# Layer 3's attention in a four-layer fp32 kernel: probabilities turned in 32x32 blocks on VectorE and placed by DMA over DRAM, values by 128 columns, order of the last heads' output

## The chip, the cores and the metric

The kernel runs on one core of one Trainium2 chip, all in fp32. The metric is the device time of one execution in microseconds. Before the change it is 3037.99 us, the median of 17 runs (3025.1 to 3042.96). Engines are named PE (TensorE; PEld are its weight loads), DVE (VectorE), ACT (ScalarE), POOL (GpSimd) and SP (SyncE, which here issues DMAs).

## The reference

Four layers, each `x = x + attention(xn) + ffn(xn)` with `xn` the layer norm of `x`: 2048 tokens of 256 values. The layers differ (a state-space mixer, latent attention with product keys, attention with few keys and a mixture of experts, and the last one). The change concerns layer 3, whose two parts are full attention with 16 heads of 128 on 4 sequences of 512 tokens, and a mixture of 8 experts:

```python
q = jnp.einsum('bpd,hde->bphe', x, W_Q) + b_Q          # k, v alike
scores = jnp.einsum('bqhe,bkhe->bhqk', q, k) / ATTN_SCALE
scores = jnp.where(causal, scores, IGNORE)
attn = jax.nn.softmax(scores, axis=-1)
z = jnp.einsum('bkhe,bhqk->bqhe', v, attn)
out = jnp.einsum('bqhe,hed->bqd', z, W_O) + b_O
# experts: out += (silu(x @ gate.T) * (x @ up.T)) @ down.T * w[:, e]
```

## The kernel before, in words

`layer3` (L2080) weaves three generators: the attention (`full_attention`, L1405), the rest of layer 2, and near the end the router of the experts. When they are done, the experts run (`SevenProductGlus.pieces`, L468). `weave` (L501) takes the next piece from the stream that is furthest behind by the costs that the pieces yield. What the pieces trace is then ordered for each engine by the tile framework, from its own estimate of when operands are ready; `tc.keep_in_program_order` pins an instruction behind the one that was traced just before it on its engine. Every engine, SP's queue of DMAs too, then runs its list in order.

The attention goes through 64 heads, n = 0 to 63 (L1555): four groups g of four heads, in each group the four sequences b, in each of these the four heads h = n mod 4. In its turn a head n does this:

- with h = 0, the values V of four heads (`values_of`, L1491): two groups of seven products of 256 columns
- the products of the next head's q and k: seven products of 256 columns each (`SevenProducts`, L282; p1 to p7 are placed by hand between the other pieces)
- the scores in four rows i of 128 queries, causal, so of 128, 256, 384 and 512 columns (`exp_scores`, L942): a matmul (L949), a DVE pass for scale, mask and minimum (L952), the exponential with its sum on ACT (L956), then reciprocal and scaling on DVE (`probabilities`, L1514, L1517 and L1518)
- for the head before it (`last`): the probabilities turned with keys on partitions (`turned`, L1521): ten 128x128 turns on PE into PSUM of tag "tr" (L1531), four copies by DVE into `PT` (L1532)
- for the head before that (`second`): the values (`values`, L1534), four matmuls of 512, 384, 256 and 128 columns (L1539), copied to `zT` by ACT (L1544); with h = 3 also the output product of four heads (`heads_out`, L960: 16 products of 256 columns, added to x by DVE at L151)

So the order on PE is, for a head without V and without output product: p1, the values of `second`, p4 of the head before, p5, the turns of 512 columns, p2, p6, then row by row scores, turns of `last`, p3 and p7. PSUM has eight banks: four of tag "mm", two of "tr", two of "acc" (`ps`, L47).

SP loads the weights of a group (`load`, L53 for wu and L1427 for wo), and waits on its queue until their places are free. Nothing else of the attention uses DMA.

The experts' stage (L468) runs 64 steps of seven products for gate and up, and interleaves the down products of the steps before as jobs (`down`, L453, `SevenSummed`, L348; each product is added to x by DVE at L461). The four last jobs follow one after the other. `hidden_sums` (L421) makes its sums on POOL.

Of the kernel before, what the change touches and what calls it, by code (L numbers as in the profile page):

```python
# [1 line left out]

# [1 line left out]

# [11 lines left out]
P = 128  # L16
# [209 lines left out]
HALF = SEQ // 2  # L226


def right_sums(c, out, blocks):

    sub = c.nc.gpsimd.tensor_sub
    (b11, b12), (b21, b22) = blocks
    sub(out[0], b12, b11)
    sub(out[1], b22, out[0])
    sub(out[2], b22, b12)
    sub(out[3], b21, out[1])
# [152 lines left out]
class SevenProductGlus:  # L391
# [26 lines left out]
        )  # L418
        return [[v[:, q, :] for v in sums] for q in range(2)]

    def hidden_sums(self, hT, q):  # L421


        t = [self.c.tile(self.pool, [P, SEQ], "hidden_sums", bufs=13) for _ in range(4)]
        (b11, b12), (b21, b22) = [[hT[half][2 * q + k] for half in range(2)] for k in range(2)]
        right_sums(self.c, t, [[b11, b12], [b21, b22]])
        hT[2].append([b11, b21, b22] + t)

    def start(self, u, p, k, hT):
# [20 lines left out]
        right = self.tokens.right(2 * p, 2)  # L450
        return SevenProducts(c, pool, left, right, out, (2, HALF), ("mm", "mm", "tr"))

    def down(self, u, p, j, hT):  # L453
# [12 lines left out]
        return SevenSummed(c, self.units[u][1], right, add, P, ("acc", "acc", "tr"))  # L466

    def pieces(self, pool):  # L468

        self.pool = pool  # L470
        n_units = len(self.srcs)
        order = [(u, p, k) for u in range(n_units) for p in range(NB // 2) for k in range(4)]
        last, jobs = None, []
        for n in range(len(order) + 6):
            now = None
            if n < len(order):
                u, p, k = order[n]
                if (p, k) == (1, 0) and u + 1 < n_units:
                    self.load(u + 1)
                if k == 0:  # L480
                    hT = [[], [], []]
                now = self.start(u, p, k, hT), u, p, k, hT
            job = self.down(*jobs.pop(0)) if jobs else None
            for mine, name, other in zip(
                (now, last, now, now, last, now, now), ("p1", "p7", "p5", "p2", "p4", "p6", "p3"),
                SevenSummed.ORDER,
            ):
                if mine:
                    getattr(mine[0], name)()
                    yield 0.87  # L490
                if job:
                    getattr(job, other)()
                    yield 0.45
                if mine and name == "p4" and mine[3] % 2 == 1:
                    self.hidden_sums(mine[4], mine[3] // 2)
            if last and last[3] == 3:
                jobs += [(*last[1:3], j, last[4]) for j in range(4)]
            last = now


def weave(c, *streams, flush=True):  # L501
# [455 lines left out]
    return pr  # L957


def heads_out(c, zT, wo, b):  # L960

    for t in range(TPB):
        po = c.ps("acc")[:, :DM]
        for h in range(4):
            c.nc.tensor.matmul(  # L965
                po, lhsT=zT[:, h, t * P : (t + 1) * P], rhs=wo[:, h, :],
                start=(h == 0), stop=(h == 3),
            )
        add_scaled(c, b * TPB + t, po)

# [434 lines left out]
def full_attention(c, a, sums, tokens):  # L1405
# [5 lines left out]
    with ExitStack() as stack:  # L1411
# [4 lines left out]
        bias = c.tile(keep, [P, 48 + DM], "bias")  # L1416
        nc.sync.dma_start(bias, a["f_small"])
        late = late_mask(c, keep, 1.0)
        units = {}

        def load(g):
# [21 lines left out]
        def projections(n):  # L1443


            g, b, h = n // 16, n // 4 % 4, n % 4
            hh = 4 * g + h
            q, k = c.tile(pool, [P, SEQ], "q"), c.tile(pool, [P, SEQ], "k")

            def out(which, bank, part):  # L1450
                to = (q, k)[which // 2][:, which % 2 * HALF : (which % 2 + 1) * HALF]
                col = which // 2 * 16 + hh
                shift = bias[:, col : col + 1]
                if part is None:
# [6 lines left out]
            return q, k, SevenProducts(c, pool, left, right, out, (HALF,))  # L1461

        def plain_projections(h):

# [26 lines left out]
        def values_of(g, b):  # L1491


            V = c.tile(pool, [P, TPB, 4, P], "V")
            right = tokens.right(b)

            def group(t):
                def out(which, bank, part):
                    col = which // 2 * 2
                    to = V[:, which % 2 * 2 + t, col : col + 2, :].rearrange("p h d -> p (h d)")  # L1500
                    if part is None:
                        nc.scalar.copy(to, bank)
                    else:
                        nc.vector.tensor_add(to, bank, part)

                return SevenProducts(
                    c, pool, units[g][2], [v[:, 0, t * P : (t + 1) * P] for v in right], out,
                    (DM,), ("mm", "mm", "acc"), swap=True,
                )

            groups = [group(t) for t in range(2)]
            return V, groups

        def probabilities(q, k, i):  # L1514
            rinv = c.tile(pool, [P, 1], "rinv", bufs=4)
            pr = exp_scores(c, pool, late, q, k, i, rinv, -scale, tc.keep_in_program_order)
            nc.vector.reciprocal(rinv, rinv)  # L1517
            nc.vector.tensor_scalar_mul(pr, pr, rinv)  # L1518
            return pr

        def turned(head, i):  # L1521

            if head is None:
                return
            if i == TPB - 1:
                head["PT"] = c.tile(pool, [P, TPB, SEQ], "PT")
            PT, pr, n = head["PT"], head["prs"][i], (i + 1) * P
            pt = c.ps("tr")
            for j in range(i + 1):
                cols = slice(j * P, (j + 1) * P)  # L1530
                tc.keep_in_program_order(nc.tensor.transpose(pt[:, cols], pr[:, cols], c.ident))  # L1531
            nc.vector.tensor_copy(PT[:, : i + 1, i * P : n], v3(pt[:, :n], P))  # L1532

        def values(head):  # L1534

            h, zT = head["h"], head["zT"]
            z = c.ps("acc")
            for j in range(TPB):
                tc.keep_in_program_order(nc.tensor.matmul(  # L1539
                    z[:, j * P :], lhsT=head["V"][:, j, h, :], rhs=head["PT"][:, j, j * P :],  # L1540
                    start=(j == 0), stop=(j == TPB - 1),
                ))
            hh = head["hh"]
            nc.scalar.activation(zT[:, h, :], z, AF.Identity, bias=bias[:, 32 + hh : 33 + hh])  # L1544
            yield 2.1
            if h == 3:
                heads_out(c, zT, head["wo"], head["b"])
                if hh == 15:
                    c.part_done(head["b"])
                yield 6.8  # L1550

        load(0)
        value_sums(0)
        second = last = None
        for n in range(64):  # L1555
            g, b, h = n // 16, n // 4 % 4, n % 4
            hh = 4 * g + h
# [7 lines left out]
            if h == 0:  # L1565
# [14 lines left out]
                zT = c.tile(pool, [P, 4, SEQ], "zT", bufs=1)  # L1580
                if b == 3 and g < 3:
                    load(g + 1)
            if (h, b) == (1, 3) and g < 3:
# [5 lines left out]
                    yield 1.7  # L1589
            else:  # L1590
                q, k, _ = ahead
            head = dict(h=h, hh=hh, b=b, V=V, zT=zT, wo=units[g][3], prs=[])
            now = None
            if 3 <= n < 63:
                ahead = projections(n + 1)
                now = ahead[2]
            if tail:
                turned(last, 3)
                yield 0.45
                for group in tail:  # L1600
                    group.p4()
                    yield 0.45
            if now:
                now.p1()
                yield 0.45
            if second:
                yield from values(second)
            if late_group:
                late_group.p4()
                yield 0.45  # L1610
            if now:
                now.p5()
                yield 0.45
            if not tail:
                turned(last, 3)
                yield 0.45
            if now:
                now.p2()
# [2 lines left out]
                yield 0.45  # L1621
            for i in range(TPB):
                head["prs"].append(probabilities(q, k, i))
                if i < 3:
                    turned(last, 2 - i)
                yield 0.7
                if now and i < 2:
                    (now.p3, now.p7)[i]()
                    yield 0.45
            second, last = last, head  # L1630
        turned(last, 3)
        yield from values(second)
        for i in range(3):
            turned(last, 2 - i)
        yield from values(last)

# [668 lines left out]
```

## Time and profile before

| what | value |
|---|---|
| median of 17 runs | 3037.99 us |
| the profiled execution's own time | 3035.4 us |
| its span, first to last instruction | 3033.6 us |
| mean granted clock of TensorE | 0.993 |
| layer 3's attention | about 1645 to 2437 us of the span |
| experts | about 2437 to 3031 us |
| DVE copies of turned rows, 128 / 256 / 384 / 512 columns (L1532) | 283 / 419 / 557 / 691 ns |
| scaling by the reciprocal, same widths (L1518) | 279 / 418 / 437 / 515 ns |
| DVE pass over the scores, same widths (L952) | 290 / 417 / 540 / 681 ns |
| exponential, same widths (L956) | 401 / 508 / 616 / 723 ns |

A row of the timeline gives start, length and what ran. Matmuls overlap, so the price of one is the step from its start to the next start, not its length. An fp32 matmul other than a turn is two instructions. "[0.96 <-DVE PT L1532]" behind a row means that its engine sat idle for 0.96 us before it, until that instruction was done. Of a DMA issue the profile gives the median time from issue to landing. The stretch view gives each engine's busy time in a stretch, the clock that TensorE was granted (1.00 is full) and what the DMAs did.

### The profile page before, as it was taken

How to read it: one execution, taken by the hardware profiler on the slowest of the kernel's cores; microseconds unless marked ns; L12 is line 12 of the kernel's file. 1: busy time of each engine (PE TensorE's matmuls, PEld its weight loads, DVE VectorE, ACT ScalarE, POOL GpSimd, SP SyncE). 2: the span in 40 equal slices, each digit the busy share in tenths (PEclk: the TensorE clock that was granted, in tenths of full speed). 3: DMA queues.
4: the chain of work that ended last, by engine and by line, in shares of the span. 5: the costliest groups of instructions: out<-in, count | busy, mean ns of one | idle time of the engine just before them, and what ended most of it. 6: DMA issues, size and time to landing. Idle time of an engine off the chain costs nothing.

```text
span 3033.6 us, 39747 instructions
## 1 busy us (share of the span) xinstructions
PE 2974.7 (98%) x13674; PEld 1962.8 (65%) x13674; DVE 2119.9 (70%) x5366; ACT 1399.9 (46%) x3336; POOL 916.9 (30%) x749
## 2 busy tenths in 40 slices
PE   8999999999999999999998999999999999999999
PEld 5666666666655555556676677777777756666666
DVE  5877877787787788787665766666666756666665
ACT  4444544444466666666523444444444433333332
POOL 0665555556210132331235200010010034333332
PEclk9999999999999999999999999999999999999999
DMA  3333333232221244443234000000000000000000
GB/s 133 94 108 122 99 97 117 85 122 88 87 66 37 64 125 102 111 105 113 85 102 128 15 1 28 1 22 8 1 21 1 22 1 22 21 21 21 22 1 29
DMA packets 89114, 185.39 MB, mean 61 GB/s; under 512 B 14192, under 2 KB 57216, under 8 KB 84176
## 3 DMA queue, kind: packets, MB, share of 16 engines
q1 hardware_dynamic: 74448, 135.05, 13.7%
q0 software_dynamic: 14176, 47.01, 6.2%
q8 instruction: 108, 1.77, 0.2%
q14 instruction: 94, 0.77, 0.1%
q10 hardware_dynamic: 288, 0.79, 0.1%
HBM read 160.92 MB, written 12.98 MB: 57 GB/s over the span
## 4 chain that ended last, share of the span: by engine, by line
PE 84%; DVE 8%; DMA 2%; ACT 2%; POOL 2%; issue 1%; SPq 0%; ACTq 0%; DVEq 0%; POOLq 0%
PE mm L301 19%; PE mm L134 14%; PE mm L949 7%; PE acc L301 6%; PE acc L1539 5%; PE acc L965 4%; PE tr L787 3%; PE tr L301 3%; PE tr L1531 2%; PE tr L1076 2%; PE mm L142 2%; PE tr L212 2%; PE acc L1212 2%; PE acc L765 2%; PE acc L212 2%; PE mm L1930 1%
## 5 line engine op out<-in xcount | busy, mean ns | idle before, releaser
L956 ACT ACTIVATE pr<-pr,nm 128x128 f32<-128x128 f32 (+3 forms) x512 | 286.3, 559 | 262.2 <-DVE nm L952 258.3
L312 ACT COPY part<-mm 128x256 f32<-128x256 f32 (+1 forms) x462 | 208.7, 459 | 231.9 <-PE mm L301 229.0
L301 PE MATMUL mm<-token_sums,unit_sums 128*128 128x512 f32 (+1 forms) x744 | 303.2, 490 | 0.0
L134 PE MATMUL mm<-xnT,wu 128*128 128x512 f32 x624 | 293.7, 608 | 3.7 <-DVE nm L952 3.6
L1330 POOL DMA_INDIRECT e<-in_p_experts,ids x128 | 129.8, 1014 | 473.9 <-DVE x L152 336.5
L952 DVE CUSTOM_DVE_ANT_0 pr<-mm,late 128x128 f32<-128x128 f32 (+3 forms) x512 | 245.4, 482 | 21.5 <-PE mm L949 18.8
L134 PE MATMUL mm<-xnT,w_in 128*128 128x512 f32 x512 | 229.2, 593 | 0.6 <-DVE cy L555 0.6
L461 DVE SCALAR_TENSOR_TENSOR x<-acc,cw,x 128x128 f32<-128x128 f32 x384 | 132.9, 346 | 112.5 <-PE acc L301 110.4
L134 PEld LDWEIGHTS mm<-xnT,wu 128*128 128x128 f32 x624 | 117.0, 195 | 127.5 <-issue 111.6
L555 DVE SCALAR_TENSOR_TENSOR cy<-mm,ws,cy 128x509 f32<-128x509 f32 (+2 forms) x216 | 160.1, 744 | 51.6 <-ACT cy L551 47.6
L949 PE MATMUL mm<-kf,qf 128*128 128x128 f32 (+3 forms) x512 | 177.1, 446 | 4.4 <-DVE qf L1053 3.8
L949 PE MATMUL mm<-k,q 128*128 128x128 f32 (+3 forms) x512 | 177.7, 436 | 1.2 <-DVE q L1478 1.2
L725 POOL TENSOR_TENSOR G<-G,CB 128x1024 f32<-128x1024 f32 x64 | 151.4, 2366 | 82.3 <-DVE G L688 76.2
L708 ACT ACTIVATE xD<-xc,ws 128x128 f32<-128x128 f32 x256 | 83.9, 390 | 193.1 <-POOL y L749 183.8
L301 PEld LDWEIGHTS acc<-down_sums,hidden_sums 128*128 128x128 f32 x768 | 114.8, 191 | 86.6 <-issue 83.7
L1532 DVE COPY PT<-tr 128x512 f32<-128x512 f32 (+3 forms) x256 | 124.6, 487 | 62.0 <-PE tr L1531 60.1
L134 PEld LDWEIGHTS mm<-xnT,w_in 128*128 128x128 f32 x512 | 96.5, 190 | 104.3 <-issue 94.7
L1539 PE MATMUL acc<-PT,V 128*128 128x512 f32 (+3 forms) x512 | 153.8, 444 | 5.0 <-DVE PT L1532 5.0
L688 DVE TENSOR_TENSOR_SCAN G<-G,eye 128x1024 f32<-128x1024 f32 x64 | 148.2, 2315 | 0.0
L1539 PEld LDWEIGHTS acc<-PT,V 128*128 128x128 f32 x512 | 93.9, 191 | 71.7 <-issue 31.7
L301 PE MATMUL mm<-xnT,wu 128*128 128x256 f32 (+1 forms) x368 | 137.0, 454 | 0.0
L444 DVE TENSOR_TENSOR whole<-mm,part 128x512 f32<-128x512 f32 x128 | 88.5, 692 | 68.4 <-PE mm L301 68.3
(408 smaller groups left out, 6720.5 us busy)
## 6 DMA issues: line engine op xcount, KB each, us to landing
G<-own SPq DMA_DIRECT2D x64, 512.0 KB, 4.2
w_in<-in_m_units SPq DMA_DIRECT2D x16, 1024.0 KB, 5.0
eb<-since SPq DMA_DIRECT2D x96, 128.0 KB, 3.3
wu<-in_o_units SPq DMA_DIRECT2D x8, 1536.0 KB, 6.4
wo<-in_m_units SPq DMA_DIRECT2D x16, 512.0 KB, 3.8
psw<-pes SPq DMA_DIRECT2D x128, 64.0 KB, 2.7
wu<-in_g_units SPq DMA_DIRECT2D x4, 1536.0 KB, 6.7
wu<-in_f_units SPq DMA_DIRECT2D x4, 1536.0 KB, 7.8
```

The lines of the kernel that those rows point to most:

```text
L134: c.nc.tensor.matmul(out, lhsT=w[:, d, cols], rhs=c.xnT[:, d, tokens], start=(d == 0), stop=(d == 1))
L301: self.c.tc.keep_in_program_order(self.c.nc.tensor.matmul(bank, lhsT=lhsT, rhs=rhs, start=first, stop=True, skip_group_check=not first))
L312: self.c.nc.scalar.copy(r, bank)
L461: c.nc.vector.scalar_tensor_tensor(x, bank, self.factor(u, tt), x, ALU.mult, ALU.add)
L555: nc.vector.scalar_tensor_tensor(y[:, j:], src[:, : SEQ - j], conv[:, k, 3 - j : 4 - j], y[:, j:], ALU.mult, ALU.add,)
L688: tc.keep_in_program_order(nc.vector.tensor_tensor_scan(flat, flat, eye.rearrange("p h t -> p (h t)"), 0.0, ALU.mult, ALU.add))
L725: nc.gpsimd.tensor_mul(G, G, seqs[b][2][:, t, :][:, None, :].to_broadcast([P, HG, P]))
L949: kept(nc.tensor.matmul(sc, lhsT=q[:, i * P : n], rhs=k[:, :n], start=True, stop=True))
L952: nc.vector.tensor_tensor_reduce(out=pr, in0=sc, in1=late[:, SEQ - n :], scale=scale, scalar=-NEG, op0=ALU.add, op1=ALU.min, accum_out=nm,)
L956: nc.scalar.activation(pr, pr, AF.Exp, bias=nm, scale=-1.0, accum_out=total)
L1330: nc.gpsimd.indirect_dma_start(out=e, out_offset=None, in_=a["p_experts"], in_offset=bass.IndirectOffsetOnAxis(ap=ids[:, t, k : k + 1], ax ...
L1539: tc.keep_in_program_order(nc.tensor.matmul(z[:, j * P :], lhsT=head["V"][:, j, h, :], rhs=head["PT"][:, j, j * P :], start=(j == 0), stop ...
```

## The change

1. **The turns.** For heads 0 to 62 PE turns nothing. After each row's scaling, DVE turns its 32x32 blocks from `pr` into an SBUF tile `Y` (`turn_blocks`; one instruction per row, of 128, 256, 384 and 512 columns). After the fourth row SP writes `Y` to DRAM in four DMAs of 32 partitions (160 KB each, in pieces of 1280 bytes), so that the blocks come to their places, and reads the whole back as `PT` in one DMA of 640 KB. The read waits for the four writes. Head 63 keeps the ten turns on PE.
2. **The values.** `PT` now lies by pairs of blocks, so the four matmuls become ten of 128 columns.
3. **Pins.** From head 5 on values are pinned; before, all were. `pr` tiles have one buffer instead of two.
4. **The order in a head.** p5 comes right behind p1 and ahead of the values. Two of the three PSUM tags of the q and k products become "tr", and one of the value projection's.
5. **The last heads.** The output products of the last group's sequences 2 and 3 are put off: their four parts are taken one by one between the last scores, values and turns.
6. **The experts' end.** The last four jobs run in two pairs, product by product, and the last `hidden_sums` is made on DVE.

```diff
-    def hidden_sums(self, hT, q):
+    def hidden_sums(self, hT, q, last):
...
-        right_sums(self.c, t, [[b11, b12], [b21, b22]])
+        right_sums(self.c, t, [[b11, b12], [b21, b22]], "vector" if last else "gpsimd")
...
-        for n in range(len(order) + 6):
+        for n in range(len(order) + 1):
...
+        while jobs:
+            both = self.down(*jobs.pop(0)), self.down(*jobs.pop(0), ("mm", "mm", "mm"))
+            for name in SevenSummed.ORDER:
+                for job in both:
+                    getattr(job, name)()
+                    yield 0.45
...
-def heads_out(c, zT, wo, b):
+def heads_out(c, zT, wo, b, done=False, kept=lambda ins: ins):
...
         add_scaled(c, b * TPB + t, po)
+        if done and t == TPB - 1:
+            c.part_done(b)
+        yield 1.7
...
-            pr = exp_scores(c, pool, late, q, k, i, rinv, -scale, tc.keep_in_program_order)
+            pr = exp_scores(c, pool, late, q, k, i, rinv, -scale, kept, bufs=1)
...
+        def blocks(ap):
+            return ap.rearrange("p (j a s) -> p j a s", a=4, s=32)
+
+        def of_row(tile, i):
+            lo = i * (i + 1) // 2
+            return tile[:, :, lo : lo + i + 1, :].rearrange("p a j s -> p j a s")
+
+        def turn_blocks(head, i):
+            if i == 0:
+                head["Y"] = c.tile(pool, [P, 4, 10, 32], "Y")
+            nc.vector.transpose(of_row(head["Y"], i), blocks(head["prs"][i]))
+            if i == TPB - 1:
+                room = c.tile(dram, [4, 32, 4, 320], "turned")
+                head["PT"] = c.tile(pool, [P, 4, 10, 32], "PT")
+                for a in range(4):
+                    nc.sync.dma_start(
+                        room[:, :, a, :].rearrange("b r e -> r b e"),
+                        head["Y"][a * 32 : (a + 1) * 32].rearrange("p b j s -> p b (j s)"),
+                    )
+                nc.sync.dma_start(
+                    head["PT"].rearrange("p a j s -> p (a j s)"), room.rearrange("b r a e -> (b r) (a e)")
+                )
+
+        def kept(ins):
+            return tc.keep_in_program_order(ins) if n >= 5 else ins
...
-            for j in range(TPB):
-                tc.keep_in_program_order(nc.tensor.matmul(
-                    z[:, j * P :], lhsT=head["V"][:, j, h, :], rhs=head["PT"][:, j, j * P :],
-                    start=(j == 0), stop=(j == TPB - 1),
-                ))
+            for i in range(TPB):
+                for j in range(i + 1):
+                    kept(nc.tensor.matmul(
+                        zs[:, i], lhsT=head["V"][:, j, h, :],
+                        rhs=head["PT"][:, :, i * (i + 1) // 2 + j, :], start=(j == 0), stop=(j == i),
+                    ))
...
             if h == 3:
-                heads_out(c, zT, head["wo"], head["b"])
-                if hh == 15:
-                    c.part_done(head["b"])
-                yield 6.8
+                b = head["b"]
+                if hh == 15 and b >= 2:
+                    put_off[b] = heads_out(c, zT, head["wo"], b, True, tc.keep_in_program_order)
+                else:
+                    yield from heads_out(c, zT, head["wo"], b, hh == 15)
...
-            if tail:
-                turned(last, 3)
-                yield 0.45
             if now:
                 now.p1()
                 yield 0.45
+                now.p5()
+                yield 0.45
+            else:
+                yield from islice(put_off.get(2, ()), 1)
             if second:
                 yield from values(second)
...
             for i in range(TPB):
                 head["prs"].append(probabilities(q, k, i))
-                if i < 3:
-                    turned(last, 2 - i)
+                if n < 63:
+                    turn_blocks(head, i)
                 yield 0.7
...
-        turned(last, 3)
+        yield from islice(put_off[2], 1)
         yield from values(second)
-        for i in range(3):
-            turned(last, 2 - i)
+        yield from islice(put_off[2], 1)
+        for i in range(TPB):
+            turned(last, TPB - 1 - i)
+        yield from put_off[2]
         yield from values(last)
+        yield from put_off[3]
```

The products and scores of the last head, and the layout of `PT` in `turned`, follow from these. In the order that the tile framework makes of the changed program, SP's queue holds, of each head, four writes and a read; the loads of the groups' weights stand between them. For most heads the read of head n stands ahead of the first write of head n+1; for n = 0, 1, 2, for h = 1 from n = 5 to 57, and for n = 60 it stands behind it.

More of the change, by code (lines that the diff above doesn't have):

```diff
@@ L1 @@
 from contextlib import ExitStack
+from itertools import islice
 import numpy as np
@@ L226, with right_sums @@
 HALF = SEQ // 2
-def right_sums(c, out, blocks):
-    sub = c.nc.gpsimd.tensor_sub
+def right_sums(c, out, blocks, engine="gpsimd"):
+    sub = getattr(c.nc, engine).tensor_sub
     (b11, b12), (b21, b22) = blocks
@@ L451, in start, with down @@
         return SevenProducts(c, pool, left, right, out, (2, HALF), ("mm", "mm", "tr"))
-    def down(self, u, p, j, hT):
+    def down(self, u, p, j, hT, tags=("acc", "acc", "tr")):
         c = self.c
@@ L465, in down @@
         right = [[v[:, j * P : (j + 1) * P] for v in hT[2][q]] for q in range(2)]
-        return SevenSummed(c, self.units[u][1], right, add, P, ("acc", "acc", "tr"))
+        return SevenSummed(c, self.units[u][1], right, add, P, tags)
     def pieces(self, pool):
@@ L494, in pieces @@
                 if mine and name == "p4" and mine[3] % 2 == 1:
-                    self.hidden_sums(mine[4], mine[3] // 2)
+                    self.hidden_sums(mine[4], mine[3] // 2, n == len(order))
             if last and last[3] == 3:
@@ L964, in heads_out @@
         for h in range(4):
-            c.nc.tensor.matmul(
+            kept(c.nc.tensor.matmul(
                 po, lhsT=zT[:, h, t * P : (t + 1) * P], rhs=wo[:, h, :],
                 start=(h == 0), stop=(h == 3),
-            )
+            ))
         add_scaled(c, b * TPB + t, po)
+        if done and t == TPB - 1:
+            c.part_done(b)
+        yield 1.7
 def latent_pieces(c, a, keep, open_pool):
@@ L1418, in full_attention @@
         late = late_mask(c, keep, 1.0)
+        dram = stack.enter_context(tc.tile_pool(name="f_dram", bufs=2, space=bass.MemoryType.DRAM))
         units = {}
@@ L1460, in projections @@
             right = [v[:, 0, :] for v in tokens.right(b)]
-            return q, k, SevenProducts(c, pool, left, right, out, (HALF,))
+            return q, k, SevenProducts(c, pool, left, right, out, (HALF,), ("mm", "tr", "tr"))
         def plain_projections(h):
@@ L1507, in group @@
                     c, pool, units[g][2], [v[:, 0, t * P : (t + 1) * P] for v in right], out,
-                    (DM,), ("mm", "mm", "acc"), swap=True,
+                    (DM,), ("mm", "tr", "acc"), swap=True,
                 )
@@ L1519, in probabilities @@
             return pr
+        def blocks(ap):
[20 more added lines that the diff above has]
+            return tc.keep_in_program_order(ins) if n >= 5 else ins
         def turned(head, i):
-            if head is None:
-                return
             if i == TPB - 1:
-                head["PT"] = c.tile(pool, [P, TPB, SEQ], "PT")
-            PT, pr, n = head["PT"], head["prs"][i], (i + 1) * P
+                head["PT"] = c.tile(pool, [P, 4, 10, 32], "PT")
+            PT, pr, w = head["PT"], head["prs"][i], (i + 1) * P
             pt = c.ps("tr")
@@ L1530, in turned @@
                 cols = slice(j * P, (j + 1) * P)
-                tc.keep_in_program_order(nc.tensor.transpose(pt[:, cols], pr[:, cols], c.ident))
-            nc.vector.tensor_copy(PT[:, : i + 1, i * P : n], v3(pt[:, :n], P))
+                kept(nc.tensor.transpose(pt[:, cols], pr[:, cols], c.ident))
+            nc.vector.tensor_copy(of_row(PT, i), blocks(pt[:, :w]))
         def values(head):
-            h, zT = head["h"], head["zT"]
-            z = c.ps("acc")
-            for j in range(TPB):
-                tc.keep_in_program_order(nc.tensor.matmul(
-                    z[:, j * P :], lhsT=head["V"][:, j, h, :], rhs=head["PT"][:, j, j * P :],
-                    start=(j == 0), stop=(j == TPB - 1),
-                ))
+            h = head["h"]
+            if h == 0:
+                if 2 in put_off:
+                    zTs.append(v3(c.tile(pool, [P, TPB, 4, P], "V").rearrange("p t h d -> p (t h d)"), SEQ))
+                else:
+                    zTs.append(c.tile(pool, [P, 4, SEQ], "zT", bufs=1))
+            zT = zTs[-1]
+            z = c.ps("acc")
+            zs = z.rearrange("p (i a s) -> p i a s", a=4, s=32)
+            for i in range(TPB):
[3 more added lines that the diff above has]
+                        rhs=head["PT"][:, :, i * (i + 1) // 2 + j, :], start=(j == 0), stop=(j == i),
+                    ))
             hh = head["hh"]
@@ L1554, in full_attention @@
         second = last = None
+        put_off, zTs = {}, []
         for n in range(64):
@@ L1579, in full_attention @@
                             yield 0.45
-                zT = c.tile(pool, [P, 4, SEQ], "zT", bufs=1)
                 if b == 3 and g < 3:
@@ L1591, in full_attention @@
                 q, k, _ = ahead
-            head = dict(h=h, hh=hh, b=b, V=V, zT=zT, wo=units[g][3], prs=[])
+            head = dict(h=h, hh=hh, b=b, V=V, wo=units[g][3], prs=[])
             now = None
@@ L1605, in full_attention @@
                 yield 0.45
+                now.p5()
+                yield 0.45
+            else:
+                yield from islice(put_off.get(2, ()), 1)
             if second:
@@ L1609, in full_attention @@
                 late_group.p4()
[L1610 to L1614, printed above, removed]
-                turned(last, 3)
                 yield 0.45
@@ L1630, in full_attention @@
             second, last = last, head
-        turned(last, 3)
+        yield from islice(put_off[2], 1)
         yield from values(second)
-        for i in range(3):
-            turned(last, 2 - i)
+        yield from islice(put_off[2], 1)
+        for i in range(TPB):
+            turned(last, TPB - 1 - i)
+        yield from put_off[2]
         yield from values(last)
+        yield from put_off[3]
 def head_mix(c, pool, w, bs):
```

## The prediction

> **What bounds the kernel now.** I read the page first (busy times, chain of waits), then layer 3's attention by stretches, then the timelines of TensorE and VectorE over one head, and last the DMA issues. An estimate below is worked out from the rows named beside it.
>
> The page's busy times and its chain of waits:
> ```profile
> PE 2974.7 (98%) x13674; PEld 1962.8 (65%) x13674; DVE 2119.9 (70%) x5366; ACT 1399.9 (46%) x3336; POOL 916.9 (30%) x749
> ...
> PE 84%; DVE 8%; DMA 2%; ACT 2%; POOL 2%; issue 1%; SPq 0%; ACTq 0%; DVEq 0%; POOLq 0%
> ```
> TensorE is both the busiest engine and 84% of the chain. In the attention it leaves almost nothing free (stretch view; columns: length, then PE, PEld, DVE, ACT, POOL busy, granted clock, DMA share, GB/s):
> ```profile
> 1700.00:2400.00 700.00, 694.49 (x3261) 537.50 (x3260) 454.29 (x1523) 310.27 (x869) 44.43 (x52) 1.00 0.03 9
> ```
> PE idles 5.5 of 700 us, VectorE is busy 65%, the DMAs 3%. So work taken off PE here shortens the kernel, until PE has to wait for something. One head on PE (timeline: start, length, line; the step from start to start is the price):
> ```profile
> 2015.78 2.42 PE L1539 MATMUL acc<-PT,V 128*128 128x512 f32 x8
> 2018.04 0.60 PE L301 MATMUL mm<-token_sums,wu 128*128 128x256 f32 x2
> ...
> 2018.91 0.60 PE L1531 MATMUL tr<-con,pr 128*128 128x128 f32 x4
> 2019.34 0.60 PE L301 MATMUL mm<-xnT,wu 128*128 128x256 f32 x2
> ...
> 2022.92 0.27 PE L1531 MATMUL tr<-con,pr 128*128 128x128 f32 x1
> 2023.03 1.02 PE L949 MATMUL mm<-k,q 128*128 128x512 f32 x2
> 2023.89 0.59 PE L301 MATMUL mm<-xnT,wu 128*128 128x256 f32 x2
> ```
> Four turns take 0.43 us (2018.91 to 2019.34), the last one 0.11; the head's ten take 1.09. A product of 256 columns (two instructions) steps by 0.43, the values by 2.26 (2015.78 to 2018.04), a short head (no value projection, no output) by 8.61 (from values at 2064.14 to values at 2072.75).
>
> **The turns leave PE.** Heads 0 to 62 lose ten each: 63 x 1.09 = **-68.7 us**, all on the bounding engine. The values become ten products of 128 columns, 20 instructions. Such instructions follow each other by 0.112 us in the last stage (four L301 products into acc, 2990.10 to 2990.55), so 2.24 against 2.26: **0** (bounds -1 and +6, should the first weight load stick out by 0.1 us in each head).
>
> Here a rule speaks against the change. The Trainium skill (VectorE: DVE Perf Modes, "The three transpose paths") gives 390 ns for a 128x128 bf16 turn on TensorE and 311 on VectorE, and its rules for authors send such turns to TensorE. By its 390 the term would be 630 x 0.39 = -246 us and the total 177 us lower; the rows' 0.109 per turn decides.
>
> **VectorE's turns.** No trace shows one. Nearest are the four copies that they replace (L1532: 0.28, 0.42, 0.56, 0.69 for 128 to 512 columns). I take those times; upper end is the slowest row by element, L688 with 2.28 us for 1024 columns, which gives 0.58, 0.86, 1.14 for 256 to 512; lower end is L1518 (0.49 for 512). VectorE has about 6.6 us of work in a short head (8.61 less 2.0 idle), and a short head will last 8.61 - 1.09 = 7.5. It fits, but its lag behind PE grows.
>
> **The new path to the values.** After the last turn SP issues four writes of 160 KB and, when they have landed, one read of 640 KB. Nearest rows:
> ```profile
> wo<-in_f_out SPq DMA_DIRECT2D x4, 512.0 KB, 3.4
> psw<-pes SPq DMA_DIRECT2D x128, 64.0 KB, 2.7
> slots_out<-os SPq DMA_DIRECT2D x22, 256.0 KB, 2.3
> wu<-in_t_shared SPq DMA_DIRECT2D x1, 768.0 KB, 4.8
> ```
> Between 512 and 768 KB the read is 3.4 + 1.4/2 = 4.1; without another load beside it I take 3.9 (ends 3.4 and 4.8). psw is also four transfers of 32 partitions; SP needs 2.41 us to issue four (1036.29), so the writes take 3 x 0.6 + 2.7 = 4.5 (slots_out, a write to DRAM, says less). Write and read: 8.5 us behind the last turn.
>
> PE reaches the values of head n one whole head after the scores of head n. With the output product (6.9 us) or the value projection (6 us) in between, that is 13.5 us or more; scores to last turn is 4.3 (below), so 4.3 + 8.5 = 12.8 just fits. For h = 1 (n = 5, 9, ... 57) both heads are short: 7.5 + 0.87. And there the order of SP's queue in the changed program is worse still: the first write of head n+1 stands **ahead of the read of head n**, and it waits for the last turn of head n+1. SP's waits show what that means: up to 196 us on one load (L53), with nothing of SP's leaving meanwhile. So the read of n leaves after the turns of n+1, while PE wants the values of n two products (0.87 us) after the scores of n+1. This holds for 14 heads, h = 1 from 5 to 57, and for 0, 1, 2 and 60.
>
> How late? VectorE after the last scores, before the change (PE goes on at 2015.29):
> ```profile
> 2015.64 0.68 DVE L952 CUSTOM_DVE_ANT_0 pr<-mm,late 128x512 f32<-128x512 f32 x1
> ...
> 2017.21 0.16 DVE L1517 RECIPROCAL rinv<-rinv 128x1 f32<-128x1 f32 x1 [0.35 <-ACT pr L956]
> 2017.41 0.49 DVE L1518 TENSOR_SCALAR pr<-pr,rinv 128x512 f32<-128x512 f32 x1
> ```
> The scaled row is there at 2017.90, 2.6 us behind. In the changed order the turns of 256 and 384 columns (0.42 + 0.56) come behind L952 too; 0.35 of it fills the wait for ACT, the copy of 0.28 in front goes, and about 0.65 of lag comes from the shorter head: 2.6 + 0.98 - 0.35 - 0.28 + 0.65 = 3.6, and the turn of 512 columns, 0.69: 4.3. Then SP's wake-up 0.1, the write in front 0.55, the read 3.9, PE's wake-up 0.1, less the 0.87 that PE still has: **8.1 us** of idle PE. Ends: 3.0 + 0.65 + 3.4 + 0.1 - 0.87 = 6.3, and 5.3 + 0.75 + 4.8 + 0.1 - 0.87 = 10.1.
>
> After such a hole the clock falls. The trace has four; this is the first (timeline, then stretch view, 0.50 is the clock):
> ```profile
> 1655.12 6.34 PE L134 MATMUL mm<-xnT,wu 128*128 128x512 f32 x8 [3.64 <-DVE nm L952]
> ```
> ```profile
> 1655.10:1660.40 5.30, 5.28 (x7) 2.16 (x8) 4.69 (x15) 3.27 (x9) 4.45 (x6) 0.50 0.34 99
> ```
> Half speed for 5.3 us costs 2.65; the others (holes of 3.88, 2.28, 2.81) have 4.5, 3.2 and 2.7 us of it. Mean 2.0, ends 1.35 and 2.65. So 14 x (8.1 + 2.0) = **+141 us** (106 to 179).
>
> Heads 0 to 2: between the scores of n+1 and the values of n stand 9 us of PE work in the built order (plain projections and scores), as long as the read needs; 0. The loads of wu and wo also move into this queue (after the writes of 14, 30, 46 and 16, 32), ahead of reads that have 10 us to spare, or 5.6 for wo against 6: under 1 us each, left out.
>
> **The other parts.** Start: PE's waits for the PT copies, 0.91 + 3.88, may go: **-4** (0 to -8, with the clock). Scattered waits in the steady part: **-3**. End of the attention: 5.8 us of waits and 1.35 of clock today; then the read of head 60, held too, costs 8.1 + 2.0, and the read of 62, behind a 1.5 MB load of weights, some 3 to 5, against which the put-off output products work: **+8** (0 to +16). End of the kernel: four jobs alone take 4.36 us each (3012.85 to 3030.4), of which 7 x 0.445 is work; in pairs the adds hide: 17.4 - 12.5, less a start: **-4** (0 to -5). hidden_sums on VectorE instead of GpSimd is in that. The changed PSUM tags fill pool places that the turns left: 0.
>
> **Sum.** -68.7 - 4 - 3 - 4 + 8 + 141 = +69 against the profiled execution's 3035.4 (span 3033.6, 1.8 around it; the median of the runs is 3038.0, 0.1% above): **3105 us**. Ends: -68.7 - 8 - 5 - 5 + 106 = +19, and -62 - 0 + 179 + 16 = +133: 3055 to 3168.
>
> The Trainium skill (DMA: Bandwidth & Descriptors, "Anatomy of one DMA — SWDGE (gpsimd) path") fits a transfer that GpSimd issues as 2.0 us plus bytes at 436 GB/s, which is 3.5 us for 640 KB. With that read the total would be 14 x 0.4 = 6 us lower; the row of 3.4 us for 512 KB, issued by SP, decides.
>
> **Rivals.**
> 1. *VectorE becomes the bound.* If a turn costs twice a copy, the head has 6.6 + 1.95 = 8.5 us of VectorE work for 7.5 of PE, and the three turns behind the last scores add 1.7 us to each of 14 holes (23 us) and up to 1 us to other short heads: 3128 to 3155. For it: 32-column pieces and fp32; against: the 35% of VectorE that is free.
> 2. *The other reads are late too.* h = 0 and 3 have 1 to 2 us to spare. With writes of 7 us (not 4.5) each waits 1 to 2 us and some fall into half clock: 30 heads x 1.5 to 2.5 give 3150 to 3180.
> 3. *Not slower.* If the read of n left ahead of the next head's write, it would land 4.3 + 8.5 = 12.8 after the scores of n, against 7.5 + 0.87: a hole of 4.4 instead of 8.1, in all about 3043. It decides from a trip of 7.6 us on (hole under 3.3, and 14 x (3.3 + 1.6) = 68.7): below, faster, down to 2957 without a hole. For it: DRAM writes of 1.8 and 2.3 us in the rows. Against: the built order itself.
>
> **Chances.** Forecast 0.66, rival 1 0.18, rival 2 0.07, rival 3 0.09 (0.07 faster, 0.02 the same). 0.2% (6 us) is about what a measurement of this kernel can tell from no change. Faster 0.07, same 0.02, slower 0.91. The range, 3055 to 3168, takes in the forecast's ends and rival 1.
>
> **What would show it.** Right: in each group of four one PE hole of 6 to 10 us ahead of the values, released by a DMA into PT, whose issue on SP comes right behind the next head's first write; clock 0.50 after it; between holes a short head in 7.5 us; turns near 0.69 us for 512 columns. The forecast is wrong if that read leaves before the next head's turns end, if the holes are under 5 us, or if PE's waits name VectorE instead.

## The result, and the profile after

| what | before | after |
|---|---|---|
| median of the runs | 3038.1 us (46 runs) | 3134.7 us (8 runs, 3130.6 to 3140.4) |
| the profiled execution's own time | 3035.4 us | 3131.3 us |
| its span | 3033.6 us | 3129.5 us |
| mean granted clock | 0.993 | 0.971 |

The ratio is 1.0322 (95% interval 1.0307 to 1.0336): slower by 3.2%. The profiled executions differ by 95.9 us; forecast were 69.

The page's busy times and its chain of waits, after:
```profile
PE 2937.1 (94%) x13812; PEld 1984.0 (63%) x13812; DVE 2120.3 (68%) x5370; ACT 1396.3 (45%) x3336; POOL 910.2 (29%) x745
...
PE 78%; DVE 11%; DMA 5%; ACT 2%; POOL 2%; issue 1%; SPq 1%; DVEq 0%; ACTq 0%; POOLq 0%
```
TensorE's share of the chain falls from 84 to 78%, and DMA's rises from 2 to 5%. The stretch that had 694.49 us of busy TensorE at full clock (length, then PE, PEld, DVE, ACT, POOL busy, clock, DMA share, GB/s):
```profile
1700.00:2400.00 700.00, 584.23 (x2932) 488.71 (x2931) 393.26 (x1318) 271.21 (x767) 44.42 (x53) 0.91 0.35 105
```
TensorE idles 116 of 700 us where it idled 5.5, and its clock is 0.91. TensorE's waits from 1690 to 2560 (waited for, us in all, times, longest) name one cause:
```profile
PE acc L1586 <- DMA PT<-turned: 133.0, 16, 10.6
PE tr L122 <- DVE q L1468: 1.8, 2, 1.3
```
One of these holes on TensorE, the values of head 33 (timeline; in brackets the idle time and who ended it):
```profile
2114.28 0.59 PE L302 MATMUL mm<-xnT,wu 128*128 128x256 f32 x2
2114.71 0.59 PE L302 MATMUL tr<-token_sums,unit_sums 128*128 128x256 f32 x2
2123.51 4.64 PE L1586 MATMUL acc<-PT,V 128*128 128x128 f32 x20 [8.21 <-DMA PT<-turned]
2127.95 0.72 PE L302 MATMUL mm<-token_sums,wu 128*128 128x256 f32 x2
```
8.21 us of nothing, and then values of 4.44 us (2123.51 to 2127.95), twice those at full clock (2.34 in the head before). SP's queue and VectorE's last turn in the same stretch:
```profile
2110.35 8.03 SPq L1550 DMA_DIRECT2D turned<-Y  x5
2118.54 0.34 SPq L1554 DMA_DIRECT2D PT<-turned  x1
2118.92 1.41 SPq L1550 DMA_DIRECT2D turned<-Y  x3
```
```profile
2117.34 0.71 DVE L1545 STREAM_TRANSPOSE Y<-pr 128x512 f32<-128x512 f32 x1
```
The page's DMA rows (number, size, median us to landing) have the writes and reads so:
```profile
turned<-Y SPq DMA_DIRECT2D x252, 160.0 KB, 2.6
PT<-turned SPq DMA_DIRECT2D x63, 640.0 KB, 3.9
```
In SP's rows, "x5" is four writes of head 33 and the first of head 34. That fifth write waits until head 34's last turn is done at 2118.05. Only then does the read of head 33 leave, at 2118.54, though its own data had been in DRAM for some 4 us. Every one of the 14 heads h = 1 from 5 to 57 has such a hole; the two other waits of more than 2 us are those of heads 60 (8.5) and 62 (2.5).

### The profile page after: what moved, and what is told of

The parts are those of the page before. It is cut to its first block, busy times and chain, and to the rows that moved or that the text cites. A ratio compares the mean times of both kernels' runs of the same rounds, so it can differ in the third digit from the quotient of the medians.

```text
span 3129.5 us, 40638 instructions
## 1 busy us (share of the span) xinstructions
PE 2937.1 (94%) x13812; PEld 1984.0 (63%) x13812; DVE 2120.3 (68%) x5370; ACT 1396.3 (45%) x3336; POOL 910.2 (29%) x745
## 4 chain that ended last, share of the span: by engine, by line
PE 78%; DVE 11%; DMA 5%; ACT 2%; POOL 2%; issue 1%; SPq 1%; DVEq 0%; ACTq 0%; POOLq 0%
PE mm L302 15%; PE mm L135 13%; PE mm L956 6%; PE acc L302 6%; PE tr L302 5%; PE acc L1586 5%; PE acc L972 3%; PE tr L794 3%; DMA PT<-turned 3%; PE tr L1086 2%; PE tr L213 2%; PE mm L143 2%; DVE pr L959 2%; PE acc L1222 2%; PE acc L772 2%; PE acc L213 2%
## 5 line engine op out<-in xcount | busy, mean ns | idle before, releaser
L1586 PE MATMUL acc<-PT,V 128*128 128x128 f32 x1280 | 185.2, 309 | 133.6 <-DMA PT<-turned 133.6
L1586 PEld LDWEIGHTS acc<-PT,V 128*128 128x128 f32 x1280 | 180.4, 223 | 143.8 <-DMA PT<-turned 141.5
L302 PE MATMUL mm<-token_sums,unit_sums 128*128 128x512 f32 (+1 forms) x624 | 267.3, 511 | 0.0
L959 DVE CUSTOM_DVE_ANT_0 pr<-mm,late 128x128 f32<-128x128 f32 (+3 forms) x512 | 244.6, 480 | 32.1 <-PE mm L956 28.7
L313 ACT COPY part<-mm 128x512 f32<-128x512 f32 (+1 forms) x372 | 175.9, 477 | 199.9 <-PE mm L302 191.8
L1468 DVE SCALAR_TENSOR_TENSOR q<-tr,bias,part 128x256 f32<-128x256 f32 x120 | 57.8, 483 | 249.6 <-PE tr L302 249.6
L462 DVE SCALAR_TENSOR_TENSOR x<-acc,cw,x 128x128 f32<-128x128 f32 x372 | 128.7, 346 | 107.1 <-PE acc L302 105.4
L956 PE MATMUL mm<-k,q 128*128 128x128 f32 (+3 forms) x512 | 172.0, 441 | 12.5 <-DVE q L1489 11.6
L1591 ACT ACTIVATE zT<-acc,bias 128x512 f32<-128x512 f32 x60 | 41.3, 688 | 226.5 <-PE acc L1586 226.5
```

The costliest lines, as they stand in the source:

```text
L302: self.c.tc.keep_in_program_order(self.c.nc.tensor.matmul(bank, lhsT=lhsT, rhs=rhs, start=first, stop=True, skip_group_check=not first))
L313: self.c.nc.scalar.copy(r, bank)
L956: kept(nc.tensor.matmul(sc, lhsT=q[:, i * P : n], rhs=k[:, :n], start=True, stop=True))
L959: nc.vector.tensor_tensor_reduce(out=pr, in0=sc, in1=late[:, SEQ - n :], scale=scale, scalar=-NEG, op0=ALU.add, op1=ALU.min, accum_out=nm,)
L1586: kept(nc.tensor.matmul(zs[:, i], lhsT=head["V"][:, j, h, :], rhs=head["PT"][:, :, i * (i + 1) // 2 + j, :], start=(j == 0), stop=(j == i),))
```

## The experiments

Theory A is that of the prediction: the reads are late because of their place in SP's queue, and a late read costs where the step to the next scores is short. Rival B: VectorE or the length of the trip makes the wait, the order does not matter. Rival C: the other reads are late too, or the DMAs slow the rest. The first four kernels ran on one chip. The others ran on chips where the kernel before took 3110 and 3100 us (in their profiles the first scores of the attention come 62 to 76 us later, with the steps behind them as on the first), so those are read by their ratio and by steps. A step, here and below, is the time from VectorE's pass over one head's row of 512 scores (L959; L952 before the change) to the same pass of the next head, where nothing else is said.

**1. The read first.** Every DMA of the turned blocks on SP is pinned:
```diff
-                    nc.sync.dma_start(
+                    tc.keep_in_program_order(nc.sync.dma_start(
...
-                nc.sync.dma_start(
+                tc.keep_in_program_order(nc.sync.dma_start(
                     head["PT"].rearrange("p a j s -> p (a j s)"), room.rearrange("b r a e -> (b r) (a e)")
```


> The changed kernel with one thing different: SP's five DMAs of a head are pinned in the order they are written, so every read of a head stands ahead of the first write of the next head; the other engines keep their order. Theory A (the place in SP's queue): the writes of a head were issued at 2110.35 to 2112.1 and take 2.6 us to land, the read then 3.9, so it lands near 2118.5 where TensorE wants it at 2115.31: holes of 3.3 us instead of 8.7 and some 2.0 us of half clock instead of 2.4, 14 x 5.8 = -81, and -5 at head 60: 3131 becomes 3045 (3035 to 3060). Rival B (VectorE's turns or the length of the trip itself makes the wait, SP's order does not matter): holes stay near 8 us and the time within 5 us of 3131.

Measured: 3050.5 us (3045.2 to 3056.3), 1.005 of before (1.0033 to 1.0067); span 3046.6. TensorE's waits, and SP's queue at heads 33 and 34:
```profile
PE acc L1586 <- DMA PT<-turned: 51.8, 16, 4.3
```
```profile
2071.30 1.77 SPq L1550 DMA_DIRECT2D turned<-Y  x4
2075.26 0.34 SPq L1554 DMA_DIRECT2D PT<-turned  x1
2078.88 1.75 SPq L1550 DMA_DIRECT2D turned<-Y  x4
```
The read now leaves ahead of the next write, 4.0 us behind its own first one. The 14 holes fall from 8.71 to 3.24 us in the mean and their half clock from 2.39 to 1.92, 83.2 us in all; the span fell by 82.9. Nothing moved but SP's order and a handful of instructions at the start of the attention. Rival B is out: the order in one queue is 83 of the 96 us lost.

**2. Heads h = 1 turned on TensorE.** With the read first, and for n = 5, 9 to 57:
```diff
+        on_pe = lambda m: m % 4 == 1 and 5 <= m <= 57
...
+            if on_pe(n - 1):
+                turned(last, 3)
...
+                if on_pe(n - 1) and i < 3:
+                    turned(last, i, "tr" if i else "mm")
...
-                if n < 63:
+                if n < 63 and not on_pe(n):
                     turn_blocks(head, i)
```


> As the run with the read first, and the heads h = 1 from 5 to 57 are turned on TensorE as before the change, so only heads with a long head behind them take the way over DRAM. Theory A: no hole is left, 14 x 11.1 and 10 at head 60 go, 14 x 1.09 of turns come back: 3131 - 155 - 10 + 15 = 2981 (2975 to 2995). Rival C (the other reads are late too, or the DMAs slow the rest): holes before the values of h = 0, 2 or 3 of 1 to 3 us, 42 of them with some half clock, 3030 and more.

Measured: 3005.9 us (3001.6 to 3013.0), ratio 0.991 (0.988 to 0.995). From 1690 to 2350 all waits for the reads are 3.6 us in 4 pieces of 1.3 us at most: apart from these the reads of h = 0, 2 and 3 are in time, so rival C is out. The time is 25 us above the number (by the profiled execution, 3001.6 us, 21). About half of that lies in the steady part: these 3.6 us, and the two heads around the turns, which step 9.65 + 6.99 us against 7.59 (first run) + 7.41 (fourth run) without them, 1.64 more and not 1.09. The other half lies at the end, where the values of heads 60 and 62 still wait 4.7 and 4.6 us.

**3. The hole filled.** 14 times, ahead of the values:
```diff
+            if h == 1 and 7 <= n <= 59:
+                for _ in range(22 if n % 16 == 15 else 17):
+                    kept(nc.tensor.matmul(
+                        v3(z[:, :256], P), lhsT=head["V"][:, 0, h, :], rhs=head["V"][:, 0, 0:2, :], start=True, stop=True,
+                    ))
```


> The changed kernel with 14 holes filled by work for nothing: ahead of the values of the heads h = 1 from 5 to 57 TensorE makes 17 products of 256 columns (22 for 13, 29 and 45) into the bank that the values then overwrite, 7.3 and 9.5 us. The wait for the read stays what it was. Theory A (the half clock behind a hole is the hole's own doing, 33.4 us over the 14): with 1 us of idle left the clock stays at 1.00 and the time falls by 33: 3098 (3092 to 3106), although TensorE does 106 us more of work. Rival D (the half clock has another cause, or the holes are not there for TensorE to use): 3131 or more.

Measured: 3105.4 us (3100.0 to 3107.8), 29 less than the changed kernel. A hole, and the stretch:
```profile
2104.01 7.50 PE L1586 MATMUL acc<-V 128*128 128x256 f32 x34
2112.46 2.50 PE L1591 MATMUL acc<-PT,V 128*128 128x128 f32 x20 [0.94 <-DMA PT<-turned]
2114.79 0.60 PE L302 MATMUL mm<-token_sums,wu 128*128 128x256 f32 x2
```
```profile
1700.00:2400.00 700.00, 684.46 (x3539) 572.27 (x3538) 410.56 (x1373) 284.24 (x805) 47.12 (x56) 1.00 0.36 109
```
The values arrive no earlier, but they take 2.33 us instead of 4.44, and the clock of the stretch is 1.00 instead of 0.91. TensorE does some 109 us more (253 products of 0.43), and the kernel is faster: the half clock is the hole's doing, and about a fifth of its price.

**4. Read first, and values late.** With the pins of the first, the values of `second` go behind the scores:
```diff
-            if second:
+            if second and not 3 <= n < 63:
                 yield from values(second)
...
+            if second and 3 <= n < 63:
+                yield from values(second)
             second, last = last, head
```


> As the run with the read first, and for heads 3 to 62 the values of the head before the last stand behind the four rows of scores of a head, where they stood ahead of them. That gives the read 3.9 us more of TensorE's work (p2, p6, p3, p7 and four rows). Theory A: 3.3 us of hole are covered, no hole and no half clock is left in the steady part: 3131 - 155 - 10 = 2966 (2955 to 2985). Rival B or C (the trip is far longer than the rows say once transfers meet, or VectorE is the bound): holes of 2 us and more stay, 3000 and above.

Measured: 2970.0 us (2966.7 to 2974.4), ratio 0.979 (0.976 to 0.982), faster than both kernels.
```profile
1750.00:2300.00 550.00, 542.51 (x2872) 455.20 (x2872) 381.27 (x1284) 274.89 (x755) 41.08 (x48) 1.00 0.43 132
```
TensorE idles 7.5 of 550 us at full clock, with the DMAs at 43%. TensorE's waits for the reads from 1690 to 2360:
```profile
PE acc L1586 <- DMA PT<-turned: 6.7, 6, 1.9
```
In this program the pins do not hold for every read: by the times of SP's rows those of heads 5, 11, 27, 43 and 58 leave behind the first write of the next head (head 11's at 1801.86, the write at 1801.39). Four of them, 5, 11, 27 and 43, are waited for, 1.1 to 1.9 us each; behind the scores of the next head stands a short step there, behind those of head 59 a long one. Four heads without such a wait take 42.95 us (13.81 + 7.41 + 14.32 + 7.41), against 47.23 before the change: 4.28 less, where four times 1.09 of turns is 4.36.

**5. Values late, SP as it comes.** The last change without the pins:

> The changed kernel with the values behind the four rows of scores of a head (heads 3 to 62), and no pins on SP. In the order that comes of it the reads of all h = 0 and h = 2 stand behind the first write of the next head, 33 in all against 18 in the changed kernel, and those of h = 1 and 3 ahead of it. Theory A, sharpened (a late read costs only where the step to the next scores is short): behind the scores of a head h + 1 = 1 or 3 comes a long step of 13.8 or 14.3 us, the read lands some 9 us behind the scores, so no hole: within 5 us of the run with both, 2970. Rival E (each read behind a waiting write costs a hole): 33 holes of some 4 us with half clock, above 3100.

Measured: ratio 0.981 (0.977 to 0.985). The steps of four heads are 13.81, 7.41, 14.32, 7.41 as in the run before, and the waits from 1720 on are few:
```profile
PE acc L1586 <- DMA PT<-turned: 7.6, 2, 6.4
```
Of 33 reads behind a waiting write (h = 0 and 2 from 0 to 60, and heads 1 and 61) 31 cost nothing. The two that do (6.4 and 1.2 us) are those of heads 61 and 60, at the end of the attention, where the work that lay between runs out. Rival E is out. A late read is no loss in itself; in the fourth run it was one only where a short step follows.

**6. Reads from GpSimd's queue.**
```diff
-                nc.sync.dma_start(
+                nc.gpsimd.dma_start(
                     head["PT"].rearrange("p a j s -> p (a j s)"), room.rearrange("b r a e -> (b r) (a e)")
```


> The changed kernel, the 63 reads issued by GpSimd's queue instead of SP's; all else the same. They wait for their own writes only. Theory A: the hole is that of the run with the read first, 3.2 us, plus what GpSimd's read takes more or less than 3.9 us, and with it the time: 3050 if it is the same, 14 us more for each us of trip. GpSimd is busy 6% here, so its waiting holds up nothing of weight. The Trainium skill (DMA: Bandwidth & Descriptors, Anatomy of one DMA, SWDGE (gpsimd) path) gives 2.0 us plus bytes at 436 GB/s, an estimate of 3.5 us for 640 KB; by it holes of 2.9 us and about 3045. Rival B (order on SP's queue doesn't matter): 3131.

Measured: ratio 1.014 (1.010 to 1.018), 0.9% or 27 us above the read first on SP. The hole of head 33 there (GpSimd, TensorE):
```profile
2161.12 0.55 POOL L1554 DMA_DIRECT2D PT<-turned  x1 [11.17 <-PE mm L302]
```
```profile
2165.33 4.12 PE L1586 MATMUL acc<-PT,V 128*128 128x128 f32 x20 [3.88 <-DMA PT<-turned]
```
Ten of the 14 holes are 3.9 us. From issue to values it is 4.2 us, against 3.9 for SP's read in the first run. The estimate of 3.5 us from the Trainium skill (DMA: Bandwidth & Descriptors, "Anatomy of one DMA — SWDGE (gpsimd) path") was too short by 0.7. One is 5.2. Three are 7.1 us, because four sums (L248 to L251, 1.3 us each) stand ahead of the read in GpSimd's own list: another queue, another wait in front. Against the first experiment the holes are 20 us longer, 12 of them in those three, and the half clock costs 5 more. For the order theory A holds; the number was 30 us too low.

**7. Turns twice.** On the kernel of the fourth run:
```diff
-            nc.vector.transpose(of_row(head["Y"], i), blocks(head["prs"][i]))
+            for _ in range(2):
+                nc.vector.transpose(of_row(head["Y"], i), blocks(head["prs"][i]))
```


> The kernel with the read first and the values late, each of VectorE's turns made twice (the second writes the same again). 2.03 us more of VectorE's work per head, 8.1 in a group of four that lasts 42.95 us and holds 30 us of VectorE's work: 89% busy. Theory A (VectorE has room in these stages): a short head lags more and the long one behind it catches up, between 2970 and 3000. Rival 1 of the prediction (VectorE is the bound as soon as a turn costs twice a copy): 28 short heads of 7.4 us become 8.7 and more, 3006 and above.

Measured: ratio 0.985 (0.981 to 0.989), some 2992 us on the first chip; VectorE is busy 81% from 1800 to 2400. VectorE falls behind in short heads (steps of 8.07 us instead of 7.41) and catches up in the long ones (13.15 and 14.01 instead of 13.81 and 14.32). Away from the waits shown next, TensorE's own steps, from scores to scores, stay 7.41 and 13.81, and 14.32 becomes 14.39 to 14.67: at most 0.35 more in four heads. TensorE's waits for the reads from 1725 to 2450:
```profile
PE acc L1587 <- DMA PT<-turned: 11.8, 4, 3.6
```
Three of the four, 2.9 to 3.6 us, are heads 11, 27 and 43, whose reads leave behind the next head's first write here too; the fourth is head 61, at the end. VectorE has the room, also at twice the price; the prediction's rival 1 is out in this order of the work.

**8. Idle work on GpSimd.** Three of the 14 holes, those of heads 13, 29 and 45, are 10.5 us long, the others 8.1 to 8.4. VectorE and GpSimd in the changed kernel, in head 46, whose last turn decides the hole of head 45:
```profile
2275.54 1.42 DVE L1529 TENSOR_SCALAR pr<-pr,rinv 128x128 f32<-128x128 f32 x1
2276.88 0.47 DVE L1468 SCALAR_TENSOR_TENSOR k<-mm,bias,part 128x256 f32<-128x256 f32 x1
2277.27 0.29 DVE L1545 STREAM_TRANSPOSE Y<-pr 128x128 f32<-128x128 f32 x1
...
2278.00 1.48 DVE L1529 TENSOR_SCALAR pr<-pr,rinv 128x256 f32<-128x256 f32 x1
```
```profile
2275.57 1.30 POOL L248 TENSOR_TENSOR unit_sums<-wu 128x512 f32<-128x512 f32 x1 [25.67 <-PE mm L302]
2276.83 1.27 POOL L250 TENSOR_TENSOR unit_sums<-wu 128x512 f32<-128x512 f32 x1
2278.07 1.26 POOL L249 TENSOR_TENSOR unit_sums<-unit_sums,wu 128x512 f32<-128x512 f32 x1
```
Each of these two scalings lasts until a sum of GpSimd's is over: 1.42 and 1.48 us where other heads show 0.28 and 0.35, 2.3 us in all, and the last turn is late by as much. The turn in between took its usual 0.29 beside L250. To test it:
```diff
+            if h == 2 and 6 <= n <= 58:
+                idle = c.tile(pool, [P, 384], "idle", bufs=1)
+                for _ in range(6):
+                    nc.gpsimd.tensor_sub(idle, k[:, :384], k[:, :384])
```


> The changed kernel, and GpSimd makes six subtractions of 384 columns for nothing, in each head with h = 2 from 6 to 58, from the moment its k is there; nothing reads their result. That is where the last turn of the row decides the length of the hole. Theory F (the three holes of 10.5 us among eleven of 8.2 come from GpSimd's four sums of 512 columns in heads 14, 30 and 46, beside which the scalings of 128 and 256 columns took 1.42 and 1.48 us instead of 0.28 and 0.35): the other eleven holes grow by 1 to 2.5 us as well, 11 to 28 us in all, and the same rows grow while the turns keep 0.30 to 0.71 us: a ratio to the changed kernel of 1.004 to 1.009. Rival G (the three long holes have another cause, such as the weights that are loaded near them): the holes stay at 8.2 us and the time within 3 us of the changed kernel's on this chip.

and beside it the changed kernel:

> The changed kernel itself, on the chip of the other two of this call, to compare them with. 1.032 of the time before, 14 holes of 8.2 and 10.5 us.

Measured: 3208.4 us against 3197.7 for the changed kernel on the same chip, ratios 1.034 (1.032 to 1.037) and 1.031 (1.029 to 1.033). The eleven holes go from 8.19 to 9.15 us in the mean, each longer than its counterpart, by 0.95, and the three others from 10.6 to 10.3. Scalings of 128, 256 and 384 columns took 0.38, 0.46 and 0.50 us in the mean instead of 0.35, 0.42 and 0.42; the turns kept 0.30, 0.44, 0.58 and 0.71. Theory F holds in kind, just under the lower end of its size: 11 x 0.95 = 10.5 us, a ratio of 1.003 between the two. The intervals of the two ratios overlap, so it rests on the holes and rows of one profile of each, where rival G had the holes stay.

**9. Read first and values late, again,** on the chip of the eighth:

> The kernel with the read first and the values late, a second time with more rounds, for the interval of what the turns on VectorE are worth once no read is late: 0.979 of the time before (0.976 to 0.982), which is the 68.7 us of turns that left TensorE, less some 3 us.

Measured: ratio 0.978 (0.975 to 0.980). This is the best version of the study: 2.2% faster than before the change, where the change itself is 3.2% slower.

## Why the prediction was right, and where it was off

Sign, mechanism and place were as forecast; the size was 27 us short. By stretches, from VectorE's pass over the 512 scores of a head to that of a later one in both profiles:

| stretch | forecast | measured |
|---|---|---|
| up to head 6: start, seven heads' turns | -4 - 7.6 = -11.6 | -7.2 |
| 6 to 54: twelve holes, idle | 12 x 8.1 = 97.2 | 105.6 |
| the same: half clock | 12 x 2.0 = 24.0 | 27.7 |
| the same: turns and scattered waits | -52.3 - 3 = -55.3 | -49.2 |
| 54 to the experts' first product with `hidden_sums`: two holes, turns, end | 20.2 - 8.7 + 8 = 19.5 | 20.5 |
| from there to the end | -4 | -1.5 |
| sum | 69.8 | 95.9 |

- *Turns leave TensorE, -68.7.* Right. The fourth experiment shows it with the holes gone: 4.28 us in four heads, and 66.2 us less of span than before. *Values by 128 columns, 0:* 2.34 us for head 32 at full clock against 2.26, within the bounds.
- *VectorE's turns like the copies.* Right: 0.30, 0.44, 0.58 and 0.71 us against 0.28 to 0.69 assumed.
- *The read held behind the next head's first write.* Right, in the 14 heads named and head 60; for 0 to 2, priced at 0, no wait of more than 0.6 us. Head 62's read has no such write ahead of it: as the prediction had it, it leaves behind a 1.5 MB load of weights (2510.14 and 2512.42); the hole is 2.5 us, not 3 to 5.
- *8.1 us of hole.* Right for eleven holes (8.14 to 8.37), in part by luck, as errors cancel. From the point where TensorE goes on to the last turn it is 3.77 us, not 4.3; wake-up and the write in front 0.49, not 0.65; but from the read's issue to the values 4.97, not 4.0; less 1.02 that TensorE still has, not 0.87. That read takes 1.0 longer than the median of 3.9 on the page. In the first experiment, where no write follows it within 2.4 us, it took 3.8 to 4.1; in the changed kernel the next head's three writes leave 0.4 us behind it. Its own trace has both: nine such reads with a recorded landing took 4.9 us in the median, thirty with no write behind them within 3 us 3.8; and writes right behind a read took 4.95 instead of 2.6. That the two slow each other is read from this, not tried apart.
- *The mean of the holes* was mis-sized: 8.71, because of the three that GpSimd lengthens (most of the 8.4 us in the table). The prediction had priced VectorE's instructions at their usual time and not looked at what else runs beside them.
- *Half clock of 2.0* was mis-sized: 2.39. The mean came from holes of 2.3 to 3.9 us; behind holes of 8 us and more the low clock held for 3.2 to 5.9 us of TensorE's work.
- *Turns and scattered waits in the steady part:* 6 us less than forecast. Besides hole and half clock, the two short heads of most groups step 7.6 to 7.9 us, where the fourth run has 7.41; what holds them there is open.
- *Start, -4:* did not come. The step that failed is "PE's waits for the PT copies, 0.91 + 3.88, may go": a wait of 9.5 us for the q of head 1 took their place. Ahead of that q on VectorE stood a scaling of 512 columns that took 4.41 us (1661.56 to 1665.97; elsewhere 0.49), while GpSimd made its sums until 1665.6. In the first experiment, with almost nothing moved there, the wait was 4.8 us: how long depends on which instructions meet.
- *End of the kernel, -4:* -1.5. The last `hidden_sums`, now on VectorE, stand between the additions of the last jobs; TensorE waits 2.34 us for one of them (L462) at 3110.65 and has half clock behind it (1.7 us), which the pairs then win back.
- *Rival 3* (read ahead of the write, "about 3043") is the first experiment: 3050.5 with holes of 3.24 us, not 4.4: the last turn comes 0.5 us earlier than reckoned, and from it to the read's issue are 4.0 us, not 4.5. That order was not in the changed kernel. (By its own sum, a hole of 3.3 us goes with a trip of 7.4 us, not 7.6.)

## What to carry to other kernels

A DMA that waits holds everything behind it in its queue, so a transfer that is ready must not stand behind one that waits for later work; and before paying for order, ask whether the consumer can come later, since the second cure alone made the order matter only at the end. Work taken off the bounding engine pays only if its replacement arrives within the time that this engine has to spare at that very place, and a hole costs more than its length: here about 2 us on top of each by the clock, for 3.2 us as for 8.7. Price a chain by what else runs beside it, not by the usual time of its instructions.

## What the runs showed of the hardware

- The half clock comes in pieces of 3.41 us (3.41, 6.83, 10.24 in the clock records). In the attention no idle time of up to 2.23 us of TensorE was followed by it in any of the profiles, apart from one of 1.33 us among longer ones, and every one of 3.13 us or more was; between, 13 were and 5 were not.
- VectorE's fp32 scaling from SBUF to SBUF is held by GpSimd's sums (1.42 us instead of 0.28 at 2275.54). From 1690 us on, 16 scalings of the changed kernel overlap a tensor-tensor instruction of GpSimd. In nine a sum runs at the scaling's recorded start or begins within 0.04 us; all nine are long (0.70 to 1.51 us instead of 0.28 or 0.35) and end 0.08 to 0.15 us behind a sum's end. Five that meet only the last 0.03 to 0.17 us of one, and two that one joins 0.07 and 0.22 us after their start, keep their time. The Trainium skill (SBUF — State Buffer, "SBUF: two separate sides") gives a reason: the two engines share a pair of ports, taken as an exclusive lock for a whole instruction by the one that starts first, and VectorE's fast two-port modes need it. The rows agree; and the 32x32 turn, which kept its time, seems not to need it.
- 640 KB read back from DRAM take 3.9 us from SP, some 5.0 with 480 KB of writes right behind, and 4.2 from GpSimd; a 160 KB write 2.6 us, 4.95 right behind such a read, and SP issues one in 0.44 us.
